# Five matmuls on ones in the hyperedges' chain, and an earlier y2T for tile 0

## The chip, the core and the metric

The kernel runs on one core of one Trainium2 chip. The metric is device time of one launch in microseconds (us), median over runs. TensorE is called PE, its weight loads PEld, VectorE DVE, ScalarE ACT, GpSimd POOL, and the queue that issues most transfers SP.

## The reference

Four layers act on x of shape (8, 2048, 64). Each computes `x = layernorm(x + layer(x))`. Two of them matter here.

Layer 0 is a graph convolution with weights of each node's own:

```
y1  = adj @ x                          # per batch
y2  = 2 * adj @ y1 - x
out = sum_d emb[n, d] * (x @ W[d,0] + y1 @ W[d,1] + y2 @ W[d,2]) + emb @ bias
```

`adj` is a 0/1 mask with its rows scaled, so the kernel multiplies by masks and scales the result.

Layer 1 is an attention over 64 hyperedges:

```
h     = x @ W
alpha = softmax over nodes of leaky_relu(h @ a_node), within each hyperedge
agg   = alpha @ h                      # one row for each hyperedge
he    = elu(agg)
se    = tanh(he @ fcW + fcb) @ av      # a score for each hyperedge
coefs1 = softmax over the hyperedges of a node, from se
industry = (adj / deg) @ (x @ W_ind)
...                                    # gates and mixes of g and industry
```

Layers 2 and 3 multiply by `adj` again.

## The kernel before

The 2048 nodes are 16 tiles of 128 rows. A tile's row holds 8 batches of 64 features, 512 columns. The two halves of a value (`hi` and `lo`) are multiplied separately.

`first_product` computes y1 of all tiles over four quarters of columns. It has eight PSUM banks: seven in the pool `acc0` (tag "acc") and one in the pool `sm0` (tag "li"). The "li" bank serves `memberships`, which makes lists of each node's hyperedges as small steps between the matmuls. When the last quarter is done, `first_product` also opens tile 0. PE multiplies y1 by tile 0's mask (`y2p_0`, line 593), ACT copies the result out, scaled, as `y2_0` (line 598), PE turns tile 0's y1 (`try1_0`, line 601) and ACT copies that out as `y1T_0` (line 606). Then the two pools close and layer 0's pools take the banks: one for `ps_acc`, one for `aggp`, two for `trs0` (tag "tr") and twice two for `pps0` (tag "pp").

Layer 0 proper (`layer0`) runs under `program_order`, which keeps each of PE, DVE, ACT and POOL in the order in which the code issues its instructions. SP's queue is not bound by it. Ahead of the loop over tiles stand these calls, with what each runs on:

- `mask(1, h)` (DVE, line 447): half of tile 1's mask from its adjacency; SP stores it for later layers.
- `scaled_first(h)` (POOL, line 1337): half h of tile 0's mask times the row scales, in two quarters `msq`.
- `compare_first(h, ...)` (DVE, line 1347): compares these two quarters with the adjacency as loaded and counts the differences into `bad`.
- `second_term(0)`: PE turns `y2_0` into a "tr" bank (four transposes, shown under line 168), and DVE subtracts x from it into `y2T_0` (line 1418).
- `summed(0, h)` (POOL, lines 1322 to 1324): additions of tile 0's mask halves, `cs`; `scaled(1, 0)` (POOL, line 1314).

The loop then calls `weigh(j, g)` for eight groups g of each tile j. A group is 12 matmuls of 256 columns (24 records in the profile, line 1448) into a "pp" buffer, from `xT`, `y1T` and `y2T` in turn; DVE then adds them into `r` with four operations (line 1459). There are two "pp" buffers, so PE's third group can begin when DVE's four operations on the first are done. Between groups 4 and 5, `visit(j)` multiplies the next tile's mask with y1 (line 1402) and does that tile's masks, comparisons and transposes.

After the last tile, `layer1` starts with what is called the head here: a chain over the 64 hyperedges, written as a list of tokens in which `c.` names a step of the chain and `1.i` four matmuls of tile 1's `industry` product (line 1928). `0.i` is the rest of tile 0's `industry` product (line 1675). `c.hexp` and `c.he` make `he` on ACT and DVE, `c.trhe` turns it on PE (four transposes), `c.heT` copies it on ACT, `c.fche` multiplies by `fcW` on PE (line 749), `c.the` is the tanh on ACT. `c.dnp` and `c.dnp2` are the weight sums on PE (line 799), 16 matmuls of 16 columns. The head's PSUM pools are `ftr` (tags "tr" and "sm", a bank each) and `fmm` (two banks).

## Time and profile before

| | us |
|---|---|
| median of 3 runs | 1196.5 |
| the three runs | 1199.98, 1196.5, 1195.7 |
| the profiled execution, its time | 1199.57 |
| the profiled execution, its span | 1197.9 |
| PE busy in the span | 1179.8 |
| mean granted clock of PE in the span | 0.993 |
| tile 0's opening: last `y2p_0` matmul started | 141.37 |
| tile 0's first group of weights started | 143.87 |
| the hyperedges' chain: `he` turned | 651.65 to 652.28 |

The span goes from the first instruction to the last. Times of single instructions are counted from its start. A row of the timeline has the start, the duration, the engine, the line, the operation, output and inputs, and in brackets how long the engine sat idle before it and who released it. PEclk is the share of the full clock that PE was granted.

### The profile page before, as it was taken

Reading aid. Unit: us, or ns where it says so; the run is one execution under the profiler, and the core shown is the slowest. Engines: PE = TensorE matmul, PEld = TensorE weight load, DVE = VectorE, ACT = ScalarE, POOL = GpSimd, SP = SyncE. Lnnn points to the kernel's source line nnn. Section 1 sums busy time; section 2 is a strip of 40 time slices with the busy share of each in tenths; the row PEclk is TensorE's granted clock in tenths of the full one; section 3 lists DMA queues with packets and bytes.
Section 4 is the critical chain, followed back from the end, with each engine's and each line's share of the span. In section 5 each row is a group of like instructions: output and inputs, shape, how many; then the busy total and the mean of one; then the engine's idle time right before and its main releaser. Section 6 shows DMA issues by size and latency. Waiting matters only on the chain.

```text
span 1197.9 us, 19875 instructions
## 1 busy us (share of the span) xinstructions
PE 1179.8 (98%) x7488; PEld 945.2 (79%) x7488; DVE 885.7 (74%) x1678; ACT 392.3 (33%) x1019; POOL 502.2 (42%) x443
## 2 busy tenths in 40 slices
PE   9999999999999999999999999999999999999996
PEld 7878788888888888888886766666667888888885
DVE  5556578888888888888877788988977666665554
ACT  3100102222222222222224467767767311111111
POOL 2000482555555555555511589988870211100000
PEclk9999999999999999999999899999999999999998
DMA  9987553323333333333385123323220433324551
GB/s 305 226 252 229 166 160 107 109 102 117 109 107 118 117 106 100 99 105 114 105 327 149 46 80 106 115 66 102 97 71 1 176 106 127 119 106 176 179 180 65
DMA packets 101991, 157.10 MB, mean 131 GB/s; under 512 B 13056, under 2 KB 64640, under 8 KB 96256
## 3 DMA queue, kind: packets, MB, share of 16 engines
q1 hardware_dynamic: 97088, 151.51, 38.3%
q10 hardware_dynamic: 4368, 4.20, 1.0%
q8 instruction: 61, 1.00, 0.4%
q0 software_dynamic: 432, 0.05, 0.1%
q14 instruction: 42, 0.34, 0.1%
HBM read 117.97 MB, written 37.76 MB: 130 GB/s over the span
## 4 chain that ended last, share of the span: by engine, by line
PE 94%; DVE 2%; DMA 1%; ACT 1%; issue 1%; POOL 0%; SPq 0%; ACTq 0%; DVEq 0%; POOLq 0%
PE pp L1448 27%; PE a L1928 19%; PE ind L1928 10%; PE y1p L567 9%; PE y2p L1402 9%; PE fc L1026 3%; PE gp L927 1%; PE try L168 1%; PE yp L2027 1%; PE trm L168 1%; PE u L1137 1%; PE dp L945 1%; PE red L976 1%; PE hp L1573 1%; PE df L691 1%
## 5 line engine op out<-in xcount | busy, mean ns | idle before, releaser
L1459 DVE SCALAR_TENSOR_TENSOR r<-pp,emb_sb,r 128x256 f32<-128x256 f32 x512 | 247.5, 483 | 74.8 <-PE pp L1448 60.7
L1448 PE MATMUL pp<-w_sb,xT 64*128 64x256 f32 x1024 | 155.4, 380 | 0.6 <-DVE r L1459 0.6
L1448 PE MATMUL pp<-w_sb,y2T 64*128 64x256 f32 x1024 | 153.4, 376 | 1.1 <-DVE y2T L1418 1.1
L1448 PE MATMUL pp<-w_sb,y1T 64*128 64x256 f32 x1024 | 153.3, 376 | 0.0
L1314 POOL TENSOR_TENSOR ms<-msk,srow 128x1024 f32<-128x1024 f32 x30 | 76.1, 2538 | 90.3 <-DVE msk L447 90.3
L1448 PEld LDWEIGHTS pp<-w_sb,y2T 64*128 64x128 f32 x1024 | 99.3, 187 | 12.7 <-DVE y2T L1418 1.6
L1448 PEld LDWEIGHTS pp<-w_sb,y1T 64*128 64x128 f32 x1024 | 99.4, 187 | 11.2
L1448 PEld LDWEIGHTS pp<-w_sb,xT 64*128 64x128 f32 x1024 | 95.1, 187 | 12.9 <-issue 2.8
L567 PE MATMUL y1p<-x_hi,m 128*128 128x512 f32 x256 | 103.3, 404 | 0.0
L567 PE MATMUL y1p<-x_lo,m 128*128 128x512 f32 x256 | 100.5, 393 | 0.2 <-DVE x_lo L470 0.2
L1928 PE MATMUL a<-y_lo,mj_l 128*128 128x512 f32 x240 | 95.0, 396 | 0.0
L1928 PE MATMUL a<-y_hi,mj_l 128*128 128x512 f32 x240 | 94.9, 396 | 0.0
L1402 PE MATMUL y2p<-y_hi,msk 128*128 128x512 f32 x240 | 94.8, 395 | 0.0
L1928 PE MATMUL a<-v_hi,mj_l 128*128 128x512 f32 x240 | 93.9, 392 | 0.0
L1928 PE MATMUL a<-v_lo,mj_l 128*128 128x512 f32 x240 | 93.7, 391 | 0.0
L1402 PE MATMUL y2p<-y_lo,msk 128*128 128x512 f32 x240 | 93.5, 389 | 0.0
L1928 PE MATMUL ind<-y_hi,mj_l 128*128 128x512 f32 x208 | 90.5, 435 | 0.0
L1928 PE MATMUL ind<-y_lo,mj_l 128*128 128x512 f32 x208 | 81.8, 393 | 0.0
L962 POOL TENSOR_TENSOR ez<-ez,coef 128x1024 f32<-128x1024 f32 x32 | 61.6, 1926 | 11.1 <-DVE ez L957 10.9
L1354 DVE SCALAR_TENSOR_TENSOR ms<-ms,adj 128x1024 f32<-128x1024 f32 x30 | 65.6, 2186 | 0.0
L1109 POOL TENSOR_TENSOR r<-r,bias_sb 128x512 f32<-128x512 f32 x14 | 17.9, 1278 | 105.3 <-DVE r L2048 105.3
L1640 POOL TENSOR_TENSOR hs<-h,es 128x512 f32<-128x512 f32 x15 | 15.6, 1043 | 107.9 <-ACT hgr L1612 107.9
(350 smaller groups left out, 2470.6 us busy)
## 6 DMA issues: line engine op xcount, KB each, us to landing
mj_l<-mask SPq DMA_DIRECT2D x44, 1024.0 KB, 4.9
adj<-in_at SPq DMA_DIRECT2D x64, 256.0 KB, 3.8
mask<-msk SPq DMA_DIRECT2D x32, 512.0 KB, 4.6
raw<-in_at SPq DMA_DIRECT2D x31, 512.0 KB, 5.8
oh<-oh SPq DMA_DIRECT2D x32, 128.0 KB, 3.0
xT<-in_xt SPq DMA_DIRECT2D x16, 256.0 KB, 3.0
xs<-in_xn SPq DMA_DIRECT2D x16, 256.0 KB, 2.7
kept<-x SPq DMA_DIRECT2D x16, 256.0 KB, 3.7
```

The costliest lines, as they stand in the source:

```text
L168: nc.tensor.matmul(dst, src, ident, start=True, stop=True, is_transpose=True)
L567: nc.tensor.matmul(accs[q][jj], r_(m[:, t, jj * P:(jj + 1) * P]), r_(part[:, mt, :]), start=i + h + t == 0 and part is x_hi, stop=i == 3 a ...
L962: nc.gpsimd.tensor_tensor(by_b(ezs[i]), by_b(ezs[i]), per_b(t["coef"], 2 * i, 2), ALU.mult)
L1026: nc.tensor.matmul(fcs[i][:, h, :], fcw_sb[rs], t["sT", i][rs], start=True, stop=True)
L1109: nc.gpsimd.tensor_tensor(b_view(t), b_view(t), bias2_sb.unsqueeze(1).to_broadcast([P, B, C]), ALU.add)
L1314: nc.gpsimd.tensor_tensor(ms, m, srow[j].unsqueeze(1).to_broadcast([P, 8, P]), ALU.mult)
L1354: nc.vector.scalar_tensor_tensor(ms, ms, 1.0, raws[j][h], op0=ALU.mult, op1=ALU.not_equal, accum_out=bad[:, 2 * j + h:2 * j + h + 1],)
L1402: nc.tensor.matmul(acc, r_(msk[j, mt // 8][:, mt % 8, :]), r_(part[:, mt, :]), start=mt == 0 and part is y_hi, stop=mt == NT - 1 and part ...
L1448: nc.tensor.matmul(pp[:, h, pl, :], terms[j][name][rs, 2 * bq + pl], w_sb[rs, k, dq * 4 * C:(dq + 1) * 4 * C], start=k == 0, stop=k == K - 1,)
L1459: nc.vector.scalar_tensor_tensor(rb, ppv[:, :, dd, :], emb_sb[:, j, d:d + 1], rb, op0=ALU.mult, op1=ALU.add)
L1640: nc.gpsimd.tensor_tensor(b_view(hs), b_view(h_sb[:, j, :]), bcast(es[:, j, :]), ALU.mult)
L1928: nc.tensor.matmul(acc, r_(a[:, mt, :]), r_(part[:, mt, :]), start=mt == 0 and part is hi, stop=mt == NT - 1 and part is lo,)
```

## The change

Three edits. In `first_product`, the bank for tile 0's y1 transposes comes from the lists' pool instead of the accumulators' pool. At the head of layer 0's loop, `second_term(0)` is called ahead of both `compare_first` calls instead of between them. In the head of `layer1`, three matmuls of a 128x128 block of ones with itself are issued ahead of the transposes of `he`, and two ahead of its product with `fcW`; they write a bank of their own, which nothing reads. All else is issued in the same order on PE, DVE, ACT and POOL. On SP's queue, the second half of tile 2's adjacency and the store of `mask(1, 1)` change places with a few small loads (`srow` of tile 3, the weights and the bias of layer 2).

```
@@ first_product
-                tr = ps_acc.tile([P, NP, P], F32, tag="acc", name="try1_0")
+                tr = ps_s.tile([P, NP, P], F32, tag="li", name="try1_0")
@@ layer1
         head = (
-            "1.mask 2.mask 3.mask 4.mask 0.i c.hexp c.he 0.ind c.trhe c.agg1 c.heT "
-            "c.fche c.sums c.the c.nagg 1.i c.sep 1.i c.serow c.sert 1.i c.ese c.eexp c.ese2 "
+            "1.mask 2.mask 3.mask 4.mask 0.i c.hexp c.he 0.ind c.w1 c.trhe c.agg1 c.heT "
+            "c.w2 c.fche c.sums c.the c.nagg 1.i c.sep 1.i c.serow c.sert 1.i c.ese c.eexp c.ese2 "
             "c.dnp c.ext 1.i c.rec c.hgr c.dnp2 1.i c.late "
         )
...
+            warm = stage1.enter_context(tc.tile_pool(name="fwm", bufs=1, space=PSUM)).tile(
+                [P, P], F32, tag="warm", name="warm_e"
+            )
+
+            def ones_twice(n):
+                for _ in range(n):
+                    nc.tensor.matmul(warm, ones, ones, start=True, stop=True)
...
                 perform(head, dict(
+                    w1=lambda: ones_twice(3), w2=lambda: ones_twice(2),
@@ layer0
             quarters = [scaled_first(h) for h in range(2)]
+            second_term(0)
             compare_first(0, quarters[0])
             mask(1, 1)
-            second_term(0)
             compare_first(1, quarters[1])
```

## The prediction

> **What bounds the kernel now.** I read the page first. TensorE is busy nearly all the span and carries the chain that ended last:

> ```profile
> PE 1179.8 (98%) x7488; PEld 945.2 (79%) x7488; DVE 885.7 (74%) x1678; ACT 392.3 (33%) x1019; POOL 502.2 (42%) x443
> ...
> PE 94%; DVE 2%; DMA 1%; ACT 1%; issue 1%; POOL 0%; SPq 0%; ACTq 0%; DVEq 0%; POOLq 0%
> ```

> So whatever moves the time delays PE, shortens one of its waits, or alters its clock. PE's list of waits is short, and the change goes at four of its lines:

> ```profile
> PE pp L1448 <- DVE y2T L1418: 1.1, 1, 1.1
> ...
> PE trhe L168 <- PE ind L1675: 0.9, 1, 0.9
> PE try L168 <- ACT y1T L606: 0.7, 1, 0.7
> PE fche L749 <- ACT heT L743: 0.7, 1, 0.7
> ```

> (Waiter, line, releaser, us in total, times, longest.) 1.8 us lie in tile 0's opening, 1.6 us in the hyperedges' chain. Next the clock, by windows. The columns are the stretch, its length, busy time of PE, PEld, DVE, ACT and POOL, and PEclk:

> ```profile
> 142.48:145.89 3.41, 1.85 (x14) 1.11 (x12) 3.41 (x4) 0.65 (x2) 3.41 (x3) 1.00 0.50 155
> 651.06:654.48 3.42, 2.15 (x10) 1.13 (x11) 3.29 (x7) 1.33 (x3) 0.00 (x0) 1.00 0.91 244
> ...
> 657.89:661.30 3.41, 3.38 (x23) 2.51 (x21) 1.49 (x8) 0.19 (x1) 0.00 (x0) 1.00 0.75 270
> ...
> 668.13:671.54 3.41, 3.41 (x7) 1.99 (x7) 2.48 (x8) 0.83 (x4) 3.09 (x3) 0.50 0.00 0
> 1186.95:1190.36 3.41, 0.96 (x9) 0.76 (x7) 2.35 (x7) 0.73 (x3) 0.00 (x0) 1.00 0.22 79
> ...
> 661.00:661.50 0.50, 0.50 (x5) 0.49 (x4) 0.00 (x0) 0.00 (x0) 0.00 (x0) 0.80 0.06 12
> 671.50:672.00 0.50, 0.50 (x3) 0.42 (x3) 0.00 (x0) 0.16 (x1) 0.00 (x0) 0.96 0.00 0
> 1190.00:1191.00 1.00, 0.00 (x0) 0.00 (x0) 0.60 (x3) 0.30 (x1) 0.00 (x0) 0.68 0.06 16
> ```

> Finally the opening of tile 0, by time on DVE, POOL and PE:

> ```profile
> 140.37 1.78 DVE L1347 SCALAR_TENSOR_TENSOR msq<-msq,adj 128x512 f32<-128x512 f32 x1
> ...
> 143.82 1.68 DVE L447 TENSOR_SCALAR msk<-adj 128x1024 fp32r<-128x1024 f32 x1
> 145.42 0.68 DVE L1418 TENSOR_TENSOR y2T<-try,xT 128x512 f32<-128x512 f32 x1
> ...
> 148.23 2.03 DVE L1459 SCALAR_TENSOR_TENSOR r<-pp,emb_sb,r 128x256 f32<-128x256 f32 x4
> ...
> 138.61 6.34 POOL L1337 TENSOR_TENSOR msq<-msk,srow 128x512 f32<-128x512 f32 x4
> ...
> 143.28 0.66 PE L168 MATMUL try<-ident,y 128*128 128x128 f32 x4 [0.68 <-ACT y1T L606]
> ...
> 146.15 0.70 PE L1448 MATMUL pp<-w_sb,y2T 64*128 64x256 f32 x4 [1.15 <-DVE y2T L1418]
> ...
> 150.57 0.60 PE L1448 MATMUL pp<-w_sb,xT 64*128 64x256 f32 x4
> ```

> DVE has no gap from 138.98 to 150.27. PE's third group of weights (150.57) needs the PSUM buffer that DVE's first four `r` (148.23 to 150.27) set free. Today that fits with 0.3 us to spare.

> **The change, part by part.** The sum is made against the profiled execution: span 1197.9, time 1199.57, so 1.67 us lie around the span. The median shown is 1196.5 (1195.7, 1196.5, 1199.98).

> *y1 turned in the lists' bank.* PE's transposes of y2 no longer wait for ACT's copy of y1T to free a bank (0.68), only for ACT's y2 (141.85 + 0.69 = 142.54), so they start at about 142.6 instead of 143.28. The first group of weights now waits for the y1T copy (142.64 + 0.59 = 143.23) because it takes the lists' bank over: 143.3 instead of 143.87. Gain here 0.6.

> *y2T ahead of both comparisons.* The transposes end at 143.26, y2T runs 143.30 to 143.98, and PE's y2T matmuls go at 144.28 instead of 146.15: gain in all 1.87. But DVE, which is in order, now idles from the mask's end (140.45) to 143.30, and five operations queue behind y2T that had stood wholly or partly ahead of it: two quarters of `compare_first(0)`, `mask(1,1)`, two quarters of `compare_first(1)`. Behind those stand the `r` that free PE's buffer. Their durations vary from 1.15 to 1.78 us, since each waits for POOL's current operation and POOL for theirs. The ends show the alternation: DVE's second quarter ends 0.51 after POOL's third; POOL's next `cs` ends 1.2 after the mask; then 0.48 (DVE), 0.65 (POOL), 0.48 (DVE), 0.38 (POOL). POOL alone needs 1.25 for a quarter, so with DVE idle its four quarters end at 144.06 instead of 144.95, and it goes on with the `cs` additions. Laid out in turns from 144.06, DVE's share 0.5 each: quarter 0.51, POOL 1.21, quarter 0.51, POOL 0.65, mask 0.51, POOL 0.38, quarter 0.50, POOL 1.21, quarter 0.50. That ends at 150.04 instead of 148.23. Four `r` at 2.03 end at 152.08, and PE's third group starts at 152.13 instead of 150.57: **1.56 slower**, although PE began it 1.9 ahead. PE stands from 148.70 (144.28 + 4.42, as today from 146.15 to 150.57) to 152.13, 3.43 us in one piece. Nothing returns this later, as PE runs without gaps through the layer's tiles. Bounds: if DVE were never held (five times 0.5), `r` would start at 146.5 and end before PE needs it: -1.9. If each of the five took its slowest pitch (1.71 four times and 1.60), `r` would start at 152.3: +3.8. I take 1.56, since the rows of these same operations alternate in this way.

> SP's queue changes too: `mask(1,1)`'s store waits for a mask that ends near 147.5 instead of 145.50, but the queue today issues it only at 149.61. The second half of tile 2's adjacency moves ahead of `srow` of tile 3, where DVE lost 3.11 us at 166.11; DVE is not the bound there. Both at nothing; without that cover the first costs what the store is late, under 1 us, and nothing before layer 1 reads it.

> *The clock in PE's new stop.* The final stop of PE (last matmul started at 1187.63) halved the clock 2.6 us later; the interrupted 142.48 window did not. A stop of 3.43 us leaves more than 2.1 us in one window for about four grid positions in five. The matmuls that follow are dense, and dense work ended the slow stretch within one window: I take 3.41 / 2 = 1.7 us. Bounds: 0 (no halving) and 10.24 / 2 = 5.1 (as long as the observed one).

> *The ones.* Three matmuls go where PE waits 0.87, two where it waits 0.68. The opening ones, 16 within 5.46 us, bound one by 0.34 from above, so three need at most 1.0 and two 0.7. By columns (a pair of 64x256 groups takes 0.43, hence one 128x128 0.21) they need 0.64 and 0.43. I take the latter, so they hide and cost 0; the upper rows would cost 0.15. They shorten no wait: `he` and `heT` come from ACT and DVE. What they can change is the clock. The slow stretch cost, by rows beside their full-clock twins: four `ind` matmuls 2.00 and 1.71 against 0.92 each (1.9), the `sx` groups 1.38 against 0.94 (0.9 for two), `gp` 1.71 against 0.92 (0.8), `dp` 1.71 against 0.86 (0.85): 4.4. The runs show the same thing: 1199.98 and 1199.57 on one side, 1196.5 and 1195.7 on the other, 3.7 apart. I take 3.7 (PE's delay is not all exposed). The grid lies anywhere against the program, so about half of the executions lose it. The ones fill the first place where a window can be thin (650.8 to 654), not the second (the weight sums at 658.4 to 661.6), from which this profile's drop came. I reckon that an execution then loses it in one of four.

> [...]

> **Sum.** 1199.57 - 3.7 (no drop in the chain) + 1.56 (third group late) + 1.7 (clock in tile 0) = 1199.1. That is 0.2% over the median shown, within the 0.5% (6 us) that a measurement of this kernel can tell from no change.

> **The rivals.**

> *The wait is simply gone* (0.13): POOL lets DVE through, `r` starts before 146.6 and the gain of 1.9 stands: 1199.57 - 3.7 - 1.9 = 1194.0. For it: POOL gets its quarters done earlier. Against: it has six `cs` additions left to alternate with.

> *The clock stays halved after tile 0's stop* (0.20). Place: the groups of weights from 152 on, 2.59 us each and dense, 5.18 at half clock. A full 10.24 us costs 5.1: 1199.57 - 3.7 + 1.56 + 5.1 = 1202.5, and 1206.2 where the chain's drop stays. It decides for "slower" from a stretch of three grid steps on. For it: the only complete slow stretch seen lasted 10.24. Against: its first two windows were full of 16-column matmuls.

> *The ones do nothing* (within the other cases): drops come from the weight sums alone. Then the time swings as before, +3.7 in half of the executions: 1202.8.

> *No halving in tile 0* (0.20): 1199.57 - 3.7 + 1.56 = 1197.4.

> **How the numbers follow.** The forecast has 0.47, the other three 0.13, 0.20 and 0.20. In each, one execution of four adds 3.7. Slower by over 0.5% (above 1202.5): half of the second rival, a quarter of the forecast, and something for a longer stop: 0.26. Faster by over 0.5% (under 1190.5) needs more than all the gains together: 0.04. The range takes in the first rival and the lower end of the second: 1194.0 to 1203.5.

> **What would show it.** In the profile after: y2 transposes near 142.6; PE's wait for y2T gone; a new wait of PE's `pp` for DVE's `r` of about 3.4 us; DVE idle for 2.9 us ahead of y2T; `r` starting near 150.0; PEclk perhaps 0.50 for 3.4 us after 150; the ones inside the two waits. I am wrong if the third group starts before 150.6, or if the clock falls in the chain as often as before.

## The result and the profile after

| | before | after |
|---|---|---|
| median, us | 1196.66 (9 runs, 1194.91 to 1199.98) | 1203.94 (9 runs, 1198.41 to 1205.28) |
| profiled execution, time / span | 1199.57 / 1197.9 | 1199.61 / 1197.9 |

The ratio after to before, from the means of the runs, is 1.0046, 95% interval 1.0028 to 1.0064: slower by about the half per cent that the forecast took as its bound. The executions of this kernel lie in groups, according to how long PE's clock was halved, so a median says little here and the groups say much. After the change three executions lie at 1198.41 to 1200.14 (mean 1199.4, mean clock 0.995 to 0.996) and six at 1202.82 to 1205.28 (mean 1204.1, clock 0.990 to 0.991). The profiled one is of the lower group.

The page of after, PE's line and the shares of the chain that ended last:

```profile
PE 1178.8 (98%) x7498; PEld 944.2 (79%) x7498; DVE 885.2 (74%) x1678; ACT 392.3 (33%) x1019; POOL 501.4 (42%) x443
...
PE 94%; DVE 3%; ACT 1%; DMA 1%; issue 1%; POOL 0%; SPq 0%; ACTq 0%; DVEq 0%; POOLq 0%
```

PE still carries the time, with ten more matmul records (the five ones, two each) and DVE's share of the chain up from 2% to 3%. The waits of PE say where. The line numbers are 8 higher in the head and 9 higher behind it:

```profile
PE pp L1457 <- DVE r L1468: 3.9, 2, 3.4
...
PE fche L757 <- ACT heT L751: 0.2, 1, 0.2
...
PE trhe L168 <- issue: 0.2, 1, 0.2
```

The four waits that the change went at are gone or short (1.1 for y2T and 0.7 for y1T no longer listed, 0.9 and 0.7 in the chain now 0.2 and 0.2), and a new one of 3.4 us stands in tile 0. The opening of tile 0 by time, on DVE, POOL and PE:

```profile
143.01 0.69 DVE L1427 TENSOR_TENSOR y2T<-try,xT 128x512 f32<-128x512 f32 x1 [2.84 <-PE try L168]
143.62 0.71 DVE L1356 SCALAR_TENSOR_TENSOR msq<-msq,adj 128x512 f32<-128x512 f32 x1
...
144.26 1.74 DVE L1356 SCALAR_TENSOR_TENSOR msq<-msq,adj 128x512 f32<-128x512 f32 x1
...
145.94 1.20 DVE L447 TENSOR_SCALAR msk<-adj 128x1024 fp32r<-128x1024 f32 x1
...
149.60 4.18 DVE L1468 SCALAR_TENSOR_TENSOR r<-pp,emb_sb,r 128x256 f32<-128x256 f32 x8
...
143.75 1.71 POOL L1331 TENSOR_TENSOR cs<-msk 128x512 f32<-128x512 f32 x1
...
142.26 0.66 PE L168 MATMUL try<-ident,y 128*128 128x128 f32 x4
...
151.78 1.23 PE L1457 MATMUL pp<-w_sb,xT 64*128 64x256 f32 x4 [3.38 <-DVE r L1468]
```

DVE stands 2.84 us ahead of y2T, then works through the comparisons. The same comparison over 128x512 takes 0.71 where POOL's four quarters end just behind its start (138.34 + 5.44 = 143.78), and 1.74 where it starts with POOL's `cs` addition under way (143.75 to 145.46); it ends 0.5 behind that addition. So `r` starts at 149.60 and PE, which had the second group behind it by about 148.4, starts the third at 151.78. The execution itself runs 0.33 us earlier here than the one of before (PE's last transpose of y1 at 142.00 against 142.33). Set against before by that amount, the third group comes 151.78 + 0.33 - 150.57 = 1.54 us later.

The clock, by windows cut along its grid. The columns are those of the prediction's windows; the last two, the DMA share and GB/s, are not used:

```profile
147.66:151.07 3.41, 0.74 (x8) 0.31 (x4) 3.34 (x7) 0.00 (x0) 3.17 (x4) 1.00 0.47 173
151.07:154.48 3.41, 2.70 (x13) 2.40 (x15) 2.46 (x6) 0.00 (x0) 3.41 (x3) 0.50 0.84 284
154.48:157.90 3.42, 3.42 (x17) 2.54 (x15) 0.55 (x2) 0.16 (x1) 3.26 (x4) 0.50 0.66 185
157.90:161.31 3.41, 3.41 (x34) 3.00 (x34) 2.07 (x5) 0.00 (x0) 3.17 (x5) 1.00 0.07 20
```

The clock is halved from the end of the window with 0.74 us of matmuls on. The next still holds 0.7 us of the stop (151.07 to 151.78), the clock stays halved through it, and it comes back at the end of the next, which is full: two windows, 6.83 us.

The half clock's price is read on PE from the third group's start to the eighth row behind it. That row, before and after:

```profile
154.00 0.60 PE L1448 MATMUL pp<-w_sb,y1T 64*128 64x256 f32 x4
...
158.22 0.60 PE L1457 MATMUL pp<-w_sb,y1T 64*128 64x256 f32 x4
```

It took 154.00 - 150.57 = 3.43 us before and 158.22 - 151.78 = 6.44 after, 3.0 more.

The position of two operations in the whole program shows what these cost. Each row has a form, its durations in ns (least, median, most), and the start of its first and last. Before:

```profile
L168 PE MATMUL trm<-ident,g x8: 270/272/273, 684.4 to 696.7; 128*128 128x128 f32 x8
...
L168 PE MATMUL trhe<-ident,he x4: 272/272/300, 651.7 to 652.0; 128*128 128x128 f32 x4
```

And after:

```profile
L168 PE MATMUL trm<-ident,g x8: 271/272/273, 684.5 to 696.8; 128*128 128x128 f32 x8
...
L168 PE MATMUL trhe<-ident,he x4: 272/273/300, 655.9 to 656.2; 128*128 128x128 f32 x4
```

At the chain's first matmuls after is 4.2 us behind, 4.5 with its earlier start: 1.54 for the third group and 3.0 for the half clock. At 684 it is level (0.1), because the execution of before lost its clock in the chain from 661.30 to 671.54, and this one of after did not. That is why the two profiled times agree while the medians are 7 us apart.

### The profile page after: what moved, and what is told of

Same layout as the page of the kernel before. It is cut to its first block, busy times and chain, and to the rows that moved or that the text cites. A ratio compares the mean times of both kernels' runs of the same rounds, so it can differ in the third digit from the quotient of the medians.

```text
span 1197.9 us, 19895 instructions
## 1 busy us (share of the span) xinstructions
PE 1178.8 (98%) x7498; PEld 944.2 (79%) x7498; DVE 885.2 (74%) x1678; ACT 392.3 (33%) x1019; POOL 501.4 (42%) x443
## 4 chain that ended last, share of the span: by engine, by line
PE 94%; DVE 3%; ACT 1%; DMA 1%; issue 1%; POOL 0%; SPq 0%; ACTq 0%; DVEq 0%; POOLq 0%
PE pp L1457 27%; PE a L1937 19%; PE ind L1937 9%; PE y1p L567 9%; PE y2p L1411 9%; PE fc L1035 3%; PE try L168 1%; PE yp L2036 1%; PE gp L936 1%; PE trm L168 1%; PE u L1146 1%; PE red L985 1%; PE hp L1582 1%; PE dp L954 1%; DVE r L1468 1%; PE df L691 1%
```

## The experiments

The theory after the result has three parts: the five DVE operations behind y2T cost 1.5 us in tile 0; the stop that they make halves the clock and costs 3.0 more; and the chain's drop of 10.24 us belongs to the weight sums, so that the ones do not prevent it, and the upper group is tile 0's halving and the chain's drop together. The rivals: the ones themselves bring the upper group; the other bank does; the chain loses its clock for another reason than the weight sums.

The table counts the executions by mean granted clock. At the end of the span 7.5 us (before, from 1190.36) and 5.8 us (after, from 1192.14) run at half clock too; in the profiles with no other drop (e2, e4, e8, e10, e11) the mean clock of 0.997 to 0.998 puts all half clock together at some 5 to 7 us. "Short" has a few us of half clock more, "long" about 10, "both" more than that. A short one is tile 0's halving in after, e1 and e9, as their profiles show; where it lies in an execution of before, no profile caught. Where an execution was not profiled, what it lost and where is read from this clock alone. "Before" is that kernel beside the experiments.

| kernel | none (0.997 up) | short (0.995, 0.996) | long (0.992 to 0.994) | both (0.991 down) |
|---|---|---|---|---|
| before (80) | 41 | 21 | 17 | 1 |
| after (9) | 0 | 3 | 0 | 6 |
| e1: y2T first and the bank, no ones (12) | 1 | 8 | 0 | 3 |
| e2: ones alone (12) | 7 | 0 | 5 | 0 |
| e3: bank alone (12) | 2 | 4 | 4 | 2 |
| e4: after, stop filled (12) | 8 | 0 | 4 | 0 |
| e5: after, sums mixed with ones (6) | 0 | 1 | 1 | 4 |
| e6: before, sums mixed with ones (6) | 0 | 3 | 2 | 1 |
| e7: y2T first, mask and comparison later (12) | 8 | 0 | 4 | 0 |
| e8: after, mask alone later (12) | 4 | 2 | 4 | 2 |
| e9: after, sums spread (6) | 0 | 3 | 3 | 0 |
| e10: e7, sums spread (12) | 3 | 6 | 3 | 0 |
| e11: e10 with ones (12) | 5 | 4 | 3 | 0 |

**e1_y2t_no_ones.** The change without its ones: tokens `c.w1` and `c.w2` left out.

```
-            "... 0.ind c.w1 c.trhe c.agg1 c.heT c.w2 c.fche ..."
+            "... 0.ind c.trhe c.agg1 c.heT c.fche ..."
```

> The changed kernel without its five ones in the chain; tile 0 as changed. Theory A (tile 0's stop of PE costs 1.5 us and then 3.4 to 5.1 us of halved clock): no better than the changed kernel, 1203 to 1206, since the stop stays and the chain's drop comes back in some executions. Theory B (the ones, or a clock drop in the chain that they bring, make the 1204 us executions): 1197 to 1199.

1199.67 us, ratio 1.003 (1.0014 to 1.0046). PE's new wait is there (3.8 us), and by their clock 11 of 12 executions have tile 0's halving: eight of them at 1199.4 on average, as the lower group of after, and three with the chain's drop too, at 1203.7. So the cost in tile 0 needs no ones.

**e2_ones_only.** Of the change only the ones.

```
-                tr = ps_s.tile([P, NP, P], F32, tag="li", name="try1_0")
+                tr = ps_acc.tile([P, NP, P], F32, tag="acc", name="try1_0")
...
-            second_term(0)
             compare_first(0, quarters[0])
             mask(1, 1)
+            second_term(0)
```

> The kernel before with the five ones alone. Theory A: 1195 to 1196.5, at or a little under the kernel before, with the chain's drop in fewer executions; PE's stop in tile 0 is not there. Theory B: most executions near 1201, 4 us over the kernel before.

1197.53 us, ratio 1.0003 (0.9986 to 1.002): the ones alone make no difference that can be seen. Five of 12 executions have the long drop, mean 1199.5; the others lie at 1196.0.

**e3_bank_only.** Of the change only the bank (`second_term(0)` put back, no ones).

> The kernel before with tile 0's y1 turned in the lists' bank alone. y2's transposes start about 0.65 us earlier, but DVE still comes to y2T only at 145.4, so PE's wait for y2T grows from 1.15 to about 1.8 us and the third group starts at 150.5 as before: within 0.3 us of the kernel before in both theories.

1198.47 us, ratio 1.0013 (0.9996 to 1.0031): no gain that can be seen. PE's wait for y2T, expected to grow to 1.8, fell from 1.1 to 0.6 in its profile, and the third group began at 149.09, which is 1.1 earlier than before when counted from PE's last transpose of y1. This profile differed from that of before in another point too (DVE's first comparison started at 138.87 against 140.37), so the 0.6 us that the bank was to bring is neither shown nor excluded.

**e4_stop_filled.** After, with 14 ones matmuls in the stop, between the second and the third group of weights, into a bank of their own.

```
                     weigh(j, g)
+                    if (j, g) == (0, 1):
+                        fill = ps_tr.tile([P, QW], F32, tag="tr", name="fill_0")
+                        for _ in range(14):
+                            nc.tensor.matmul(fill[:, 0:P], ones, ones, start=True, stop=True)
```

> The changed kernel with 14 more matmuls on ones (0.21 us each, 3.0 us) between PE's second and third group of weights, where it stands 3.4 us. Theory A: the third group still starts near 151.8, but the clock stays full: 1197.5 to 1199 in nearly all executions. Theory B: unchanged, two executions of three near 1204.

1198.22 us, ratio 1.0017 (1.0003 to 1.0031). PE is busy in the stop, and the third group comes late all the same:

```profile
149.73 3.39 PE L1813 MATMUL fill<-ones 128*128 128x128 f32 x28
153.67 0.70 PE L1457 MATMUL pp<-w_sb,xT 64*128 64x256 f32 x4 [0.55 <-DVE r L1468]
```

The rows after it are at full clock (0.43 us apart), and by their clock no execution of 12 has the halving. Eight lie at 1197.65 on average, which is 1.8 above the executions of before without a drop in the same batch (1195.84): the price of the late third group by itself (1.54, and the third group comes another 0.5 later here: 4.47 us behind the last row of the second, against 3.98 in after). Four have the long drop, at 1201.2. Against the lower group of after (1199.4) the filled stop gives back 1.7, the half clock's price less that half microsecond, and somewhat less than the rows say (3.0 - 0.5). The upper group of after is gone with tile 0's halving, which fits two drops in one execution; the profile of e5_sums_filled below shows both.

**e7_compare_later.** The order that keeps y2T first without the queue behind it: `mask(1, 1)` after the first group of weights, the second comparison after the fourth; no ones.

```
             second_term(0)
             compare_first(0, quarters[0])
-            mask(1, 1)
-            compare_first(1, quarters[1])
...
                     weigh(j, g)
+                    if (j, g) == (0, 0):
+                        mask(1, 1)
+                    elif (j, g) == (0, 3):
+                        compare_first(1, quarters[1])
```

> The changed kernel without its five ones, with mask(1, 1) put behind DVE's additions of the first group of weights and compare_first(1) behind those of the fourth. Only compare_first(0) stands between y2T and the first additions, which then start near 146.3; PE's third group follows the second without a stop, 1.9 us ahead of the kernel before. Theory A: 1194.0 in the executions without a drop, 0.997 or 0.998 in about half of all, no drop in tile 0; median 1194 to 1196. Rival (DVE makes up for it later, PE stops at a later group): 1196 or more, with PE's waits for r adding up to over 1.5 us.

1195.23 us, ratio 0.9998 (0.9984 to 1.0013). By its timeline (DVE, then PE) `r` now follows two quarters of the comparison only, and PE's stop is short:

```profile
146.68 2.03 DVE L1468 SCALAR_TENSOR_TENSOR r<-pp,emb_sb,r 128x256 f32<-128x256 f32 x4
...
148.86 0.70 PE L1457 MATMUL pp<-w_sb,xT 64*128 64x256 f32 x4 [0.27 <-DVE r L1468]
```

The third group is at 148.86 instead of 151.78; counted from PE's last transpose of y1 it is 1.56 earlier than before. By their clock no execution has the short drop. The eight without a drop lie at 1194.67, 0.9 below those of before in the same batch (1195.54), but they scatter from 1193.25 to 1197.39, so that the times alone don't show a gain. Where DVE's queue doesn't let PE go on, y2T first costs some 4.5 (1.54 and the half clock's 3.0). Four of 12 have the long drop, and over all executions the time is level with before.

**e8_mask_later.** After, with only `mask(1, 1)` moved, as in e7_compare_later.

> The changed kernel with mask(1, 1) alone put behind DVE's additions of the first group. DVE's additions start 1.1 us earlier (about 148.5), PE's stop ahead of its third group shrinks from 3.4 to about 2.3 us. Theory A: the third group starts near 150.6, as in the kernel before, and the halving in tile 0 is seen in fewer executions than the changed kernel's nine of nine: 1196 without any drop, 1197.5 with tile 0's. Rival (any stop of this size halves the clock): 0.995 or less in nearly all executions, 1198.3 and more.

1198.44 us, ratio 1.0021 (1.0005 to 1.0038). `r` at 148.14, PE's stop 1.9 us in its profile, the third group level with before (0.07 later, counted as above): half the way between after and e7_compare_later. By their clock at most four of 12 executions had the halving in tile 0, against all nine with a stop of 3.4.

**e5_sums_filled and e6_sums_filled_alone.** A ones matmul after every second weight sum, in after and in before, to keep the window of the sums busy.

```
                         nc.tensor.matmul(...)   # a weight sum
+                        if j % 2:
+                            ones_twice(1)
```

> The changed kernel with one more matmul on ones (0.21 us) after every second weight sum of the chain, eight in all, about 1.7 us of PE's time. The executions of the changed kernel near 1204 lose 10 us more of full clock than those near 1199.4. Theory A (that loss starts in the weight sums, whose window is thin): all executions near 1199.4 + 1.7 = 1201, with a mean clock of 0.995 to 0.996, none at 0.991. Theory B (it is a longer halving in tile 0): two of three still at 0.991 and near 1205.

> The kernel before with these eight ones among the weight sums alone, without the five of the change. Of 35 executions of the kernel before, 18 have a mean clock of 0.997 or 0.998 (mean 1195.8), 9 have 0.995 or 0.996 (1197.6), 8 less (1200.1 and more). Theory A (the long loss is the weight sums', the short one the chain's two waits'): the long ones go, the short ones stay in about a quarter; 1197.5 and 1199.3. Theory B (both come from the two waits): the shares stay as before.

1206.48 us, ratio 1.0084 (1.0067 to 1.01), and 1202.38, ratio 1.0058 (1.0036 to 1.008). Both missed what was hoped of them: the drop stayed, by the clock in five of six executions of e5_sums_filled and three of six of e6_sums_filled_alone. Its timeline on PE shows why:

```profile
662.36 0.35 PE L807 MATMUL dnp<-ese,pT 64*128 64x16 f32 x2
662.64 0.49 PE L722 MATMUL warm_e<-ones 128*128 128x128 f32 x2
663.06 0.38 PE L807 MATMUL dnp<-ese,pT 64*128 64x16 f32 x2
```

A pair of sums with its ones takes 0.70 us (662.36 to 663.06) where four sums took 0.51 before, so the filling only made the stretch longer. The windows of the same execution, one with both drops, show both halvings in one run:

```profile
149.70:153.12 3.42, 0.36 (x4) 0.40 (x6) 3.21 (x7) 0.00 (x0) 3.18 (x5) 1.00 0.44 142
153.12:156.53 3.41, 3.41 (x20) 3.21 (x18) 1.53 (x4) 0.00 (x0) 3.33 (x3) 0.50 1.01 317
...
665.12:668.53 3.41, 3.41 (x19) 2.72 (x20) 0.00 (x0) 0.00 (x0) 0.00 (x0) 1.00 0.02 5
668.53:671.94 3.41, 3.41 (x13) 3.00 (x13) 1.22 (x3) 0.32 (x1) 0.00 (x0) 0.50 0.00 0
```

In tile 0 the stop ended near the grid's edge (153.12), so one full window brought the clock back: 3.41 us here, 6.83 in after. In the chain the clock fell after a window that is busy from end to end, with nothing in it but 19 records of sums and ones.

**e9_sums_spread, e10_later_spread, e11_later_spread_ones.** The 12 later weight sums cut into three parts of 4 with tile 1's `industry` matmuls between, in after, in e7_compare_later, and in the latter with the ones.

```
-            "c.dnp c.ext 1.i c.rec c.hgr c.dnp2 1.i c.late "
+            "c.dnp c.ext 1.i c.rec c.hgr c.dnp2 1.i c.dnp2b 1.i c.dnp2c c.late "
...
-            "... 1.sx 0.ch0 0.m0 1.i 1.ST "
+            "... 1.sx 0.ch0 0.m0 1.ST "
```

> The changed kernel, with the 12 later weight sums cut into three parts of 4 and a matmul of tile 1's gates work between each two, so that the 16-column matmuls no longer fill a window of 3.41 us between them. Theory A (the long drop in the chain comes from the weight sums' window; the ones stand elsewhere and don't touch it): the drop after the weight sums is gone, tile 0's halving stays in nearly every execution, all executions near 1199.4, none at 1204: 1199.4 median. Theory B (the long drop belongs to the chain as a whole, or follows from the ones): 1204 stays in half or more of the executions.

> The kernel with y2T first and the second half of the mask and the second comparison later (e7_compare_later, no ones), and with the weight sums spread as in e9_sums_spread. Theory A: no long drop and no halving in tile 0; what remains of drops is the short one of about 2 us in the chain's waits, in about a quarter of the executions if the ones are what removes it: 1194.7 without, 1196.5 with, median 1194.9. Theory B: long drops in a third of the executions as in e7_compare_later, 1199.

> As e10_later_spread, with the ones in the chain's two waits as in the change. Theory A: no drop of any length except the one at the end; every execution within 0.5 of 1194.8, faster than before by 0.1 to 0.2%. Theory B (the ones bring drops nearer, since with ones 21 of 45 executions had the long drop and without 24 of 93): long drops in about half the executions, 1199; e10_later_spread has fewer of them.

1200.19, 1196.67 and 1196.88 us; ratios 1.0042 (1.0026 to 1.0059), 1.0005 (0.9996 to 1.0013) and 1.0007 (0.9995 to 1.0019). In e9_sums_spread none of six executions has a clock of 0.991 or less, against six of nine in after. But only part of what was expected came: by their clock three have tile 0's halving alone (mean 1200.0) and three some us of half clock more (mean 1201.7). The slowest, 1203.58, still lies in the range of after's upper group, so a drop remained; that it became shorter is read from the clock of three executions and was not seen in a profile. In e10_later_spread the three longest executions are 2.1 us above its three without a drop (1197.7 against 1195.57), where before's long ones in the same batch are 3.5 above (1198.4 against 1194.9). The spreading may cost something: PE's `sx` has a new wait of 0.4 us for ACT in all three profiles, and the three executions of e10_later_spread without a drop are 0.7 above before's, while those of e7_compare_later were 0.9 below; three executions don't settle it.

In e10_later_spread no execution is above 1197.83, where before's go up to 1199.26, and the mean is level with before. With the ones the median is the same (1196.88 against 1196.67), but three of 12 executions are above 1199. Where the remaining drops of e9_sums_spread to e11_later_spread_ones lie was not caught in a profile: the three profiles show no drop in the chain.

**What the weight sums do to a window**, by the busy time of their line alone (columns: the stretch, its length, PE, PEld, clock, DMA). Before, in the window that the drop followed:

```profile
657.89:661.30 3.41, 1.87 (x16) 1.81 (x16) 1.00 0.75 270
```

e7_compare_later, in the window that the drop of its profile followed:

```profile
656.85:660.26 3.41, 2.08 (x16) 1.93 (x16) 1.00 0.57 203
```

After, in the two windows over which its sums lie, with no drop behind either:

```profile
659.66:663.07 3.41, 0.47 (x4) 0.50 (x4) 1.00 1.02 282
663.07:666.48 3.41, 1.61 (x13) 1.42 (x13) 1.00 0.40 145
```

Sixteen records of the sums lay in one window, with 1.5 (before) and 1.3 us (e7) of it for all other matmuls, and the clock fell. Split 4 and 13 (one counted twice at the edge), it didn't. In e9_sums_spread, where parts of four records (0.58 to 0.61 us each) start 1.63 to 1.68 us apart, the clock stays at 1.00 from 655 to 671. The edge at which the long drop began was read in four profiles: in before (661.30) and e5 (668.53) it lies within the sums, in e6 (664.97) and e7 (660.26) 0.08 and 0.12 us behind the end of their last row. So in these profiles it is where the grid lies against the sums that goes with the loss of the clock; the executions without a profile were not seen.

## Why the prediction was right and wrong

**Tile 0's turn-taking of DVE and POOL: right.** DVE's second comparison and its mask ended at 146.00 and 147.14, 0.54 and 0.56 behind POOL's first two `cs` (145.46, 146.58). The third group came 1.54 us later where 1.56 was worked out, `r` started at 149.60 + 0.33 = 149.93 (150.04), PE stood 3.38 (3.43), DVE idled 2.84 (2.9), and the transposes of y2 started 0.26 after the last of y1's, with no wait. The rival "the wait is simply gone" fell by the row that was held against it: POOL's `cs` additions are there to alternate with.

**The half clock after the new stop: that it came was right, its size wrong.** The term was 1.7 (one window). It measured 3.0, over two windows (6.83 us), where the rival of a longer stretch had three (5.1). The step that failed is "dense work ended the slow stretch within one window". In after the window in which the stop ends, with 2.70 us of matmuls, did not bring the clock back, and the next, with 3.42, did: two windows. In e5_sums_filled and e9_sums_spread the first window of the stretch was full (3.41), and it lasted one (e9's by its mean clock of 0.996). In the chain of before all three windows were recorded as full (3.41 and 3.42), and the clock came back at the end of the third; the first two held some 1.6 and 1.3 us of 16-column matmuls (0.29 of the sums, the rest `sx`), so they were not full of them. The grid lay elsewhere in each execution: an edge stands at 149.31 in before, at 151.07 in after, at 149.70 in e5 and at 150.02 in e9. By the clock it came in all nine executions, not in four grid positions of five.

**The chain's drop: its price right, its chance wrong.** Priced at 3.7, from the displacement it is 4.2 - 0.1 = 4.1, and between the groups of after 4.7. The step that failed is "I reckon that an execution then loses it in one of four". The reckoning was a half without the ones and a quarter with them. In the runs 31 of 116 executions without the ones had it (before, e1, e3, e7: 27%) and 21 of 45 with them (after, e2, e4, e8: 47%); six of nine in after. The prediction's own sign of being wrong, "if the clock falls in the chain as often as before", has therefore come: it fell more often. The prediction had seen that the drop comes from the weight sums and not from the waits that the ones fill, and still counted half of the drops as prevented. That the ones make it more frequent is not shown: before alone has 18 of 80, but the changed kernels without the ones (e1, e3, e7) have 13 of 36, which is not far from 21 of 45. Why six of nine had it in after, and so why the median fell into the upper group, stays open: the counts are small, the kernels differ in tile 0 too, and the sums spread brought no answer. Executions with a short drop are absent in e2 and e4 (0 of 24, before 21 of 80), which could have been a service of the ones; e11 with four of 12 speaks against it, and e7 has none without any ones.

**The number.** Forecast 1199.1 for executions without the chain's drop and 1202.8 with it; measured 1199.4 and 1204.1. That the lower one fits is in part luck. Against the profiled execution (1199.61) the half clock was put 1.3 too low, and most of that is taken back: 0.4 too little was taken off for the chain's drop, and this execution started 0.33 earlier. The median is 4.8 above the forecast since it fell into the other group, just over the upper end of the range (1203.5). "Within half a per cent" was given 0.70 and "slower" 0.26; the ratio of 1.0046 lies on the first side, its interval on both.

**The ones cost nothing: right.** The delay in tile 0's opening (4.2 at the first `y2p` matmul behind tile 0's weights, 163.06 against 158.84) is still 4.2 at `trhe`, with three ones ahead of it: PE's wait there fell from 0.87 to 0.20, so they took 0.67 (0.64), and the two ahead of `fche` took 0.45 (0.43). e2_ones_only is level with before.

## What to carry to other kernels

Moving y2T to the front of DVE's order put the five operations that it overtook behind it, and `r` started at 149.60 instead of 148.23: look at what stands between the moved operation and the next one that another engine waits for, and move those too (e7_compare_later, `r` at 146.68). Here a stop of the tensor engine that took 2.7 of a clock window's 3.41 us cost more through the clock than through the wait, 3.0 us for a delay of 1.5. Filler matmuls helped in the stop itself (e4_stop_filled: 1.7 us back, no halving by the clock of 12 executions), and not among the small matmuls (e5_sums_filled and e6_sums_filled_alone: a drop in five and three of six).

## What the runs showed that was not expected

The clock fell after windows recorded as full: 3.38 of 3.41 us in before and e7, where the 16-column weight sums took 1.87 and 2.08, and 3.41 in e5 and e6, where sums and ones took turns. Where PE simply stood, the clock was halved behind windows with 0.00 (after, at the end of the span), 0.36 (e5), 0.74 (after), 0.96 (before, at the end) and 1.38 us (e9) of matmuls, and it stayed full behind windows with 1.85 (before), 1.86 (e9) and 1.99 us (e5). The slow stretches followed to their end by windows lasted 3.41 (tile 0 in e5), 6.83 (after) and 10.24 us (the chain in before and e5).

A 128x128 ones matmul took 0.24 us in the dense filling of e4_stop_filled (3.39 for 14) and, from its start to the next row's, 0.42 between 16-column matmuls in e5_sums_filled (662.64 to 663.06): a filler's price depended on its neighbours.
